# One graph-network layer on one core: the two half-block transfers of x and of the result become one, and ScalarE asks for x

## The chip, the cores and the metric

The kernel runs on one core of one Trainium2 chip. The metric is the device time of a launch in microseconds, and where several runs were made, their median. A core has five engines with instruction streams of their own: TensorE (PE; its weight loads are listed apart as PEld), VectorE (DVE), ScalarE (ACT), GpSimd (POOL) and SyncE (SP). SP, ACT and POOL can ask for transfers; the transfers themselves run on 16 DMA engines that all three share.

## The reference: what is computed

There are 12,500 nodes with 128 numbers each (`x`), and 412,500 edges with 48 numbers each (`edge_attr_48`), sorted by the node that receives them (`dst`). Cut to what matters, the reference is:

```python
h = jnp.maximum(_layernorm(x, axis=-1), 0.0)
agg = jax.ops.segment_sum(edges, dst, num_segments=12500)   # 12500 x 48
u = graph_globals[0]                                        # the same 64 numbers for all nodes
z = jnp.concatenate([h, agg, u], axis=1)
return x + (jax.nn.relu(z @ W1 + b1) @ W2 + b2)             # W1: 240 x 256, W2: 256 x 128
```

So every node is normalized, gets the sum of its edges' numbers beside it, and goes through a two-layer network; the result is added to `x`. All numbers are float32. The edges are 79.2 MB, `x` and the result 6.4 MB each.

## The kernel before, in words

**Two streams.** The edges are cut into 403 chunks of 1,024 edges (128 partitions x 8), and the chunks into two halves, the streams. A step takes one chunk of each stream; 6 steps make a group (`CG`), and there are 34 groups and 207 steps. In a step `contract` (L370) multiplies, for each of 8 edges per partition and for both streams, 48 edge columns with a one-hot matrix, which adds them up by receiver in PSUM (L377; a float32 product leaves two records in the trace, so a step shows 32). VectorE builds the one-hot matrices a group ahead (`onehot`, L365), and `add` (L393) adds a finished group into the big sums `aggT` in SBUF. Stream 0 lies on partitions 0 to 47 and stream 1 on 64 to 111.

**Node blocks.** The first 6,144 nodes belong to stream 0, and as many from node 6,356 (`END`) on to stream 1. Both are cut into 25 blocks. A block has 64 partitions (`PH`) of each stream, and each partition holds r nodes that follow one another in memory: r is 2 in the first and the last block and 4 in the other 23. So one partition's part of `x` is one run of 2 KB (1 KB where r is 2). The 212 nodes between the streams are a 26th block of 53 partitions. A block goes through these parts, which `pieces` and `parts` put between the steps: `normalization` (L483: `bn_stats` on DVE at L517, some small DVE and ACT operations, `xn` on ACT at L513), `transpose` (L524, copied to `hT` by ACT at L533), `hidden_x` and `hidden_sums` (L537 and L556, with the result taken by ACT as `hid` at L573), `output` (L577, products at L585), and `store` (L590: DVE adds `x` and the bias into `ot`, L593, and SP stores it, L598).

**Transfers.** SP asks for all edges (`load_edges`, L151): a transfer brings two chunks, and 15 buffers are filled ahead (`PF`); after that, a new load follows each pair of chunks that has been used up. SP also asks for most of `dst` (L180) and stores the results, all in one order. POOL asks for the weights, the biases and `x`. Two of the small ones tell something of how a transfer is spread: SP's very first one, `first0` (L250), fetches four numbers as a 1 x 2 x 2 pattern, and ACT's first two, `di` (L180), fetch 12 rows of 4 KB each.

**How x is asked for.** `load_x(k)` (L207) takes a buffer for a pair of blocks and puts one `load` per block on a list with the step from which it is due; there are four such buffers (`XBUFS`). `next_x` (L231) takes the next due one off the list and emits it; it is called every third step. For a block, `load` emits two transfers, one for the 64 partitions of each stream (L218). `store` does the same with the result:

```python
for s in range(2):
    nc.sync.dma_start(rows_of(out, s * END + a0, PH, nr), od[s * PH:(s + 1) * PH])
```

Before the first step, POOL asks for the first three blocks of `x` (L304, L308 and L316), between clearing `aggT` and loading the weights.

**Spare products.** `stir(n)` (L333) multiplies the identity with itself n times into a PSUM tile that nobody reads (L336). It is called with 4, 5 and 3 ahead of the first step, and in the steps before the 14th wherever no piece was taken (L741).

Of the kernel before, what the change touches and what calls it, by code (L numbers as in the profile page):

```python
# [21 lines left out]
def kernel(  # L22
# [31 lines left out]
    nc = tc.nc  # L54
    N, D = x.shape
# [32 lines left out]
    XBUFS = 4  # L88
    PH = P // 2
# [11 lines left out]
    END = MID + NM  # L101
# [67 lines left out]
    def next_edges():  # L169
        if e_loads:  # L170
            _, s, c, n = e_loads.pop(0)
            e = ep.tile([P, CL, T * DE], F32, name="e")
            load_edges(e, c, n)
            for k in range(n):
                edges[c + k] = (e[:, k], k == n - 1)

    def load_chunks(di, at, c, n, queue):

        full = max(0, min(n, NFULL - c))
        queue.dma_start(di[at:at + full], dst[c * CE:(c + full) * CE].rearrange("(c e) -> c e", e=CE))  # L180
        if full < n:
            for q in range(0, CE, TAIL):
                m = min(TAIL, CE - q)
                queue.dma_start(di[at + full:at + n, q:q + m], dst[None, E - m:E])

    def rows_of_block(b):

        return [sum(chunks[s * NI + begins[b]:s * NI + begins[b + 1]]) for s in range(2)]
# [3 lines left out]
    def load_dst(b, queue):  # L192
        di = dp.tile([P, CE], I32, name="di", bufs=2)
        at = 0
        for s, n in enumerate(rows_of_block(b)):
            load_chunks(di, at, C0[s] + begins[b] * CG, n, queue)
            at += n
        return di

    def rows_of(ap, a, m, r):  # L200

        return ap[a:a + m * r].rearrange("(p r) d -> p (r d)", p=m)

    xs, xts, xns, xbs, hTs, hids, pos = {}, {}, {}, {}, {}, {}, {}
    x_loads = []

    def load_x(k):  # L207

        if k >= len(pairs):
            return  # L210
        xt = xp.tile([P, 2, R * D], F32, name="xt")
        xts[k] = xt

        def load(i, j):
            a, m, r = blocks[j]
            if j < NB2:
                for s in range(2):
                    nc.gpsimd.dma_start(xt[s * PH:(s + 1) * PH, i, :r * D], rows_of(x, s * END + a, PH, r))  # L218
                return
            f = m - m % 16  # L220
            nc.gpsimd.dma_start(xt[:f, i, :r * D], rows_of(x, a, f, r))
            if f < m:
                nc.gpsimd.dma_start(xt[f:m, i, :r * D], rows_of(x, a + f * r, m - f, r))

        for i, j in enumerate(pairs[k]):
            xs[j] = xt[:, i].rearrange("p (r d) -> p r d", d=D)
            x_loads.append((k, lambda i=i, j=j: load(i, j), max(step, min(16 * k - 32, 114 + 4 * k))))
# [3 lines left out]
    def next_x(late=0):  # L231

        if x_loads and x_loads[0][2] <= step - late:
            k, load, _ = x_loads.pop(0)
            load()
            came[k] = step
# [11 lines left out]
    with nc.allow_non_contiguous_dma(reason="a few hundred numbers, once"):  # L248
        begin = begins[1]
        nc.sync.dma_start(  # L250
            first0, dst[:2 * C0[1] * CE].rearrange("(a s e) -> a s e", a=1, s=2)[:, :, GE // 2:begin * GE:GE])
    dis = {0: load_dst(0, nc.scalar)}
    for i in range(PF):
        next_edges()
        if i == 1:
            dis[1] = load_dst(1, nc.sync)
# [19 lines left out]
    with nc.allow_non_contiguous_dma(reason="a few hundred numbers, once"):  # L276
        for s in range(2):
            mid0 = C0[s] * CE
            n = min(NI, (E - mid0) // GE)
# [3 lines left out]
            for i in range(n, NI):  # L283
                m = mid0 + i * GE + GE // 2
# [13 lines left out]
        at += n  # L298
    for c in range(0, 2048, 1024):
        nc.gpsimd.memset(aggT[:, c:c + 1024], 0.0)  # L300
    step = -4
    for k in range(XBUFS):
        load_x(k)
    next_x()  # L304
    nc.gpsimd.memset(w1a, 0.0)
    with nc.allow_non_contiguous_dma(reason="a few hundred numbers, once"):
        nc.gpsimd.dma_start(w1h, W1[0:D])
        next_x()  # L308
        nc.gpsimd.dma_start(w1u, W1[D + DE:D + DE + G])
        nc.gpsimd.dma_start(u, graph_globals[0:1].rearrange("a g -> g a"))  # L310
        nc.gpsimd.dma_start(b1_sb, b1.rearrange("(a p) -> p a", p=P))
        nc.gpsimd.dma_start(w1a[0:DE], W1[D:D + DE])
        nc.gpsimd.dma_start(w1a[HI:K2], W1[D:D + DE])
        nc.gpsimd.dma_start(w2, W2.rearrange("(a p) d -> p a d", p=P))
        nc.gpsimd.dma_start(b2_sb, b2[None, :].to_broadcast([P, D]))
    next_x()  # L316
    for c in range(2048, NC, 1024):
        nc.gpsimd.memset(aggT[:, c:min(c + 1024, NC)], 0.0)
    least = const.tile([1, NG], F32)
# [13 lines left out]
    def stir(n):  # L333

        for _ in range(n):
            nc.tensor.matmul(spare[:, 0], ident, ident, start=True, stop=True)  # L336
# [58 lines left out]
    def first_nodes(b):  # L395

        at = 0
        for s, n in enumerate(rows_of_block(b)):
            g = s * NI + begins[b]
            m = -(-n // CG)  # L400
            nc.vector.tensor_tensor(
                brow[:, b, at:at + m * CG].rearrange("a (i k) -> a i k", k=CG),
                offs[:, None, :].to_broadcast([1, m, CG]),
                (first[:, g:g + m] if b else first0[:, s])[:, :, None].to_broadcast([1, m, CG]), OP.subtract)
            at += n
# [8 lines left out]
    def shift_dst(b, di):  # L414

        rows = rows_in[b]
        ra, rb = rows_of_block(b)
        pb = pst.tile([P, 2], F32, name="pt")
        nc.tensor.matmul(pb[:rows, 0:1], brow[:, b, :rows], one, start=True, stop=True)  # L419
        nc.tensor.matmul(pb[:rows, 1:2], (cols if b < NB - 1 else last_cols)[:, :rows], one, start=True, stop=True)  # L420
        nc.scalar.copy(base[:rows, b], pb[:rows])  # L421
        df = dp.tile([P, CE], F32, name="df", bufs=2)
        nc.scalar.activation(df[:rows], di[:rows], AF.Identity, bias=base[:rows, b, 0:1])
        return df

    def spread(b, df, parts=(0, 1), start=False):

        ra, rb = rows_of_block(b)
        if 0 in parts:
            rels[b] = dp.tile([P, IB, CG // 2, 4 * T], F32, name="rel", bufs=2)  # L430
            if b == NB - 1:
                nc.gpsimd.memset(rels[b][:, NI - 1 - begins[b]], 0.0)
        rv = rels[b].rearrange("p i h (k s t) -> p s t (i h k)", s=2, t=T)
        q = T // 2
        for t0 in [a * q for a in parts]:
            own = start and t0
            pt = turn_dst(df, ra + rb, t0, *((psh, "ph") if own else (pst, "pt")))
            nc.scalar.copy(rv[:, 0, t0:t0 + q, :ra], pt[:, :, :ra])
            (nc.vector.tensor_copy if start else nc.scalar.copy)(rv[:, 1, t0:t0 + q, :rb], pt[:, :, ra:ra + rb])  # L439
# [150 lines left out]
    def store(j):  # L590
        a0, m, nr = blocks[j]
        ot = mp.tile([P, R, D], F32, name="ot")
        nc.vector.tensor_tensor(ot[:m, :nr], pos.pop(j)[:m, :nr], xbs.pop(j)[:m, :nr], OP.add)  # L593
        k = m - m % 16
        od = ot[:, :nr].rearrange("p r d -> p (r d)")
        if j < NB2:
            for s in range(2):
                nc.sync.dma_start(rows_of(out, s * END + a0, PH, nr), od[s * PH:(s + 1) * PH])  # L598
            return
        nc.sync.dma_start(rows_of(out, a0, k, nr), od[:k])  # L600
        if k < m:
            nc.scalar.dma_start(rows_of(out, a0 + k * nr, m - k, nr), od[k:m])
# [17 lines left out]
    pieces = [(8, 0.4, lambda: turn(0)), (12, 0.8, lambda: turn(1))]  # L620
# [37 lines left out]
    def turn(j):  # L658
        nonlocal turned
        while not normalized(j):  # L660
            next_part(True)
        transpose(j)
        turned = j
# [12 lines left out]
    stir(4)  # L676
    first_nodes(0)
    dfs = {0: shift_dst(0, dis[0])}
    stir(5)
    spread(0, dfs[0], start=True)  # L680
    stir(3)
# [17 lines left out]
    for b in range(1, NB):  # L699
        i = begins[b]  # L700
# [15 lines left out]
    for step in range(CG * NI + 3):  # L716
        i, k = divmod(step, CG)
        if i < NI:
            contract(i, k)
        for f in plan.get(step, []):  # L720
            f()
        if step % 3 == 2:
            next_x(1)
        if k == 0:
            if i > 0:
                add(0, i - 1)
                add(1, i - 1)
        if k == 0:
            hots.pop(i - 1, None)
            onehot(i + 1, (0, 2))  # L730
        if k == 2:
            onehot(i + 1, (1,))
        store_late()
        for _ in range(2 if step % 2 or step < 20 else 1):
            next_part()
        credit = min(credit + 0.75, 1.2)
        n = len(pieces)
        while pieces and pieces[0][0] <= step and pieces[0][1] <= credit:
            credit -= pieces[0][1]
            pop_piece()  # L740
        if n == len(pieces) and step < 14:  # L741
            stir(1)
    while pieces:
        pop_piece()
        store_late()
# [114 lines left out]
```

## Time and profile before

| | us |
|---|---|
| median of 3 runs | 372.35 (370.56 to 373.52) |
| the profiled execution, its own time | 373.86 |
| its span, first to last instruction | 372.1 |
| PE busy | 325.3 (87%) |
| DVE busy | 242.0 (65%) |
| ACT busy | 123.8 (33%) |
| POOL busy | 42.2 (11%) |

The mean granted TensorE clock was 0.969 of full speed. The profile is of one execution; its own time stands 1.5 us above the median of the runs, and its span 1.8 us below its own time. The rows of the page say how long an engine was busy in the whole span; a row of "busy tenths" divides the span into 40 slices of 9.3 us. A group row names the line, the engine, the operation, what it writes and reads, and how often; then its busy time, the mean of one, and the idle time ahead of it with what ended most of it. Transfers are listed by queue: q1 is SP's, q10 is ACT's, q0 is POOL's, and q8 and q14 bring instructions; a packet is one run of bytes or one 4-byte receipt that a DMA engine writes when its share of a transfer is done.

### The profile page before, as it was taken

What the parts mean: (1) busy time and instruction counts of PE and PEld (TensorE: products, weight loads), DVE (VectorE), ACT (ScalarE), POOL (GpSimd) and SP (SyncE); (2) the same over time, 40 slices, a digit from 0 to 9 for tenths busy, and PEclk for the clock granted to TensorE, in tenths of its full rate; (3) what the DMA queues carried; (4) which work ended last, traced back from release to release, by engine and by line L of the source; (5) the groups of instructions that cost most, each with busy time, mean ns of one, the idle gap of its engine ahead of it and who ended that gap; (6) DMA issues with size and microseconds to landing.
All of it is one profiled execution on the core that took longest, in us unless ns stands there. A gap on an engine that the chain in (4) does not pass through costs nothing.

```text
span 372.1 us, 17860 instructions
## 1 busy us (share of the span) xinstructions
PE 325.3 (87%) x8059; PEld 261.5 (70%) x8060; DVE 242.0 (65%) x415; ACT 123.8 (33%) x296; POOL 42.2 (11%) x106
## 2 busy tenths in 40 slices
PE   7878968799986986999996986999999999999981
PEld 7766757787875765886874865777787778687661
DVE  2987555495992766776497582866868877785310
ACT  3224323085041072072242051543062335412330
POOL 9670400020020020020020020010000010000000
PEclk9997989899998999999999999999999999999996
DMA  7999999999898799899779899898889798941021
GB/s 214 307 315 307 326 304 309 307 320 315 272 306 246 233 291 285 271 296 317 227 239 313 267 282 264 267 300 261 286 256 307 238 343 269 307 150 36 21 53 29
DMA packets 62285, 95.41 MB, mean 256 GB/s; under 512 B 5277, under 2 KB 57097, under 8 KB 62198
## 3 DMA queue, kind: packets, MB, share of 16 engines
q1 hardware_dynamic: 59340, 87.16, 76.0%
q0 software_dynamic: 2800, 6.90, 7.3%
q8 instruction: 65, 1.06, 1.2%
q14 instruction: 22, 0.18, 0.2%
q10 hardware_dynamic: 58, 0.11, 0.1%
HBM read 87.74 MB, written 6.40 MB: 253 GB/s over the span
## 4 chain that ended last, share of the span: by engine, by line
PE 80%; issue 10%; DVE 5%; ACT 2%; POOL 0%; DVEq 0%; ACTq 0%; POOLq 0%
PE ps L377 40%; PE po L585 12%; PE ph L553 11%; PE ph L566 7%; PE pt L529 4%; PE po L336 3%; DVE oh L365 3%; PE pt L445 1%; ACT hid L573 1%; DVE ot L593 1%; DVE aggT L393 1%; DVE st L517 0%; ACT xn L513 0%; PE pt L419 0%; PE pt L420 0%
## 5 line engine op out<-in xcount | busy, mean ns | idle before, releaser
L377 PEld LDWEIGHTS ps<-oh,e 128*48 128x48 f32 x6448 | 180.9, 128 | 76.6 <-issue 69.7
L377 PE MATMUL ps<-oh,e 128*48 128x44 f32 (+1 forms) x6448 | 193.5, 219 | 25.4 <-issue 25.1
L365 DVE TENSOR_TENSOR oh<-iota,rel 128x2816 f32<-128x2816 f32 (+3 forms) x72 | 149.8, 2099 | 6.7 <-ACT rel L439 5.7
L573 ACT ACTIVATE hid<-ph,bias 128x256 f32<-128x256 f32 (+2 forms) x102 | 41.6, 460 | 87.7 <-PE ph L566 85.8
L393 DVE TENSOR_TENSOR aggT<-aggT,ps 48x201 f32 (+1 forms) x68 | 24.4, 359 | 65.3 <-PE ps L377 51.8
L585 PE MATMUL po<-w,hid 128*64 128x128 f32 (+1 forms) x784 | 60.9, 280 | 6.7 <-issue 6.0
L553 PE MATMUL ph<-hT,w1h 128*64 128x512 f32 (+2 forms) x208 | 55.4, 586 | 1.1 <-issue 1.1
L218 POOL DMA_DIRECT2D xt<-in_x_dram x50 | 26.0, 528 | 236.2 <-ACT xn L513 76.0
L585 PEld LDWEIGHTS po<-w,hid 128*64 128x64 f32 (+1 forms) x784 | 44.9, 138 | 9.7 <-issue 7.4
L513 ACT ACTIVATE xn<-xt,sh,sc 128x128 f32<-128x128 f32 (+1 forms) x100 | 42.7, 488 | 2.8 <-DVE sh L507 2.8
L593 DVE TENSOR_TENSOR ot<-po,xb 128x512 f32<-128x512 f32 (+2 forms) x26 | 17.4, 670 | 33.1 <-PE po L585 32.8
L566 PE MATMUL ph<-aggT,w1a 48*64 48x256 f32 (+1 forms) x400 | 32.5, 393 | 3.6 <-ACT hid L573 3.5
L503 ACT ACTIVATE sc<-va,eps 128x8 f32<-128x8 f32 (+3 forms) x15 | 4.5, 299 | 84.2 <-DVE va L502 84.2
L517 DVE BATCH_NORM_STATS2 st<-xt 128x6 f32<-128x128 f32 (+1 forms) x100 | 23.2, 279 | 0.0
L533 ACT COPY hT<-pt 128x512 f32<-128x512 f32 (+2 forms) x26 | 14.4, 554 | 16.6 <-PE pt L529 16.5
L529 PE MATMUL pt<-ident,xn 128*128 128x128 f32 (+1 forms) x100 | 17.3, 297 | 0.0
L566 PEld LDWEIGHTS ph<-aggT,w1a 48*64 48x64 f32 x400 | 10.6, 131 | 8.3 <-ACT hid L573 4.7
L547 DVE TENSOR_TENSOR xb<-xt,b_sb 128x1024 f32<-128x1024 f32 (+3 forms) x15 | 15.6, 1037 | 0.1
L553 PEld LDWEIGHTS ph<-hT,w1h 128*64 128x64 f32 x208 | 12.4, 141 | 2.5 <-issue 2.4
L336 PE MATMUL po<-ident 128*128 128x128 f32 x46 | 12.2, 402 | 2.0 <-POOL ident masks.py:199 2.0
L529 PEld LDWEIGHTS pt<-ident,xn 128*128 128x128 f32 (+1 forms) x100 | 10.9, 147 | 1.7 <-issue 0.4
L421 ACT COPY base<-pt 108x2 f32<-108x2 f32 (+3 forms) x5 | 0.8, 156 | 30.6 <-PE pt L420 30.6
(92 smaller groups left out, 101.0 us busy)
## 6 DMA issues: line engine op xcount, KB each, us to landing
e<-in_edge_attr_dram SPq DMA_DIRECT2D x200, 384.0 KB, 5.3
xt<-in_x_dram POOLq DMA_DIRECT2D x46, 128.0 KB, 7.2
out_dram<-ot SPq DMA_DIRECT2D x46, 128.0 KB, 3.2
di<-in_dst_dram SPq DMA_DIRECT2D x4, 216.0 KB
e<-in_edge_attr_dram SPq DMA_DIRECT2D x2, 192.0 KB, 4.0
di<-in_dst_dram SPq DMA_DIRECT2D x2, 180.0 KB
di<-in_dst_dram SPq DMA_DIRECT2D x2, 144.0 KB
xt<-in_x_dram POOLq DMA_DIRECT2D x4, 64.0 KB, 5.3
```

The lines of the kernel that those rows point to most:

```text
L218: nc.gpsimd.dma_start(xt[s * PH:(s + 1) * PH, i, :r * D], rows_of(x, s * END + a, PH, r))
L336: nc.tensor.matmul(spare[:, 0], ident, ident, start=True, stop=True)
L365: nc.vector.tensor_tensor(hots[i][:, at:at + n * Q * w].rearrange("p (h q w) -> p h q w", h=n, w=w)[:, :, q], iota[:, None, None, :w].to_b ...
L377: nc.tensor.matmul(ps[s * HI:s * HI + DE, o:o + WID[k]], edges[c][0][:, t * DE:(t + 1) * DE], hot(i, s, k, t), start=(k == 0 and t == 0), ...
L393: nc.vector.tensor_tensor(to, to, acc[i % len(acc)][h, :wg], OP.add)
L513: nc.scalar.activation(xns[j][:m, r], xs[j][:m, r], AF.Relu, bias=sh[:m, c:c + 1], scale=sc[:m, c:c + 1])
L517: parts.append((k, None, lambda i=i, j=j, r=r: nc.vector.bn_stats(st[:m, i * nr + r, :], xs[j][:m, r, :])))
L529: nc.tensor.transpose(pt[:, r, :m], xn[:m, r], ident[:m, :m])
L553: nc.tensor.matmul(phs[j, a][c:c + HI, :nr * m], w1h[:, a * P + c:a * P + c + HI], hTs[j], start=True, stop=False, skip_group_check=True)
L566: nc.tensor.matmul(phs[j, a][c:c + HI, s * n:(s + 1) * n], w1a[h, a * P + c:a * P + c + HI], aggT[h, f:f + n], start=False, stop=True, ski ...
L573: nc.scalar.activation(hids[j][:, a, :nr, h:f], phs[j, a][:, h * nr:f * nr].rearrange("h (p r) -> h r p", r=nr), AF.Relu, bias=bias[:, a:a ...
L585: nc.tensor.matmul(pos[j][c:k, r], hids[j][:, a, r, c:k], w2[:, a], start=(a == 0), stop=(a == NH - 1), skip_group_check=True)
```

## The change

A helper `both` describes the rows of both streams of one block as one pattern in device memory: 2 streams, `END * 128` numbers apart, by 64 partitions by one run of r x 128 numbers. With it, a block of `x` is one transfer into 128 partitions and no longer two into 64, and a block of the result one transfer out of 128 partitions. `x` is asked for by ScalarE and no longer by GpSimd. The first three blocks of `x` are no longer asked for between POOL's start-up work: their calls come after `shift_dst` of the first part of `dst`, so in ACT's order behind the first two of its operations there (L421, L423). The spare products inside the steps are dropped; the 12 ahead of the first step stay. SP still stores the results, and the 53-partition block keeps its two transfers of 48 and 5 partitions.

```diff
+    def both(ap, a, r):
+
+        return bass.AP(tensor=ap.tensor, offset=ap.offset + a * D, ap=[[END * D, 2], [r * D, PH], [1, r * D]])
+
...
             a, m, r = blocks[j]
             if j < NB2:
-                for s in range(2):
-                    nc.gpsimd.dma_start(xt[s * PH:(s + 1) * PH, i, :r * D], rows_of(x, s * END + a, PH, r))
+                nc.scalar.dma_start(xt[:, i, :r * D], both(x, a, r))
                 return
             f = m - m % 16
-            nc.gpsimd.dma_start(xt[:f, i, :r * D], rows_of(x, a, f, r))
+            nc.scalar.dma_start(xt[:f, i, :r * D], rows_of(x, a, f, r))
             if f < m:
-                nc.gpsimd.dma_start(xt[f:m, i, :r * D], rows_of(x, a + f * r, m - f, r))
+                nc.scalar.dma_start(xt[f:m, i, :r * D], rows_of(x, a + f * r, m - f, r))
...
     dis = {0: load_dst(0, nc.scalar)}
+    step = -4
+    for k in range(XBUFS):
+        load_x(k)
...
-    step = -4
-    for k in range(XBUFS):
-        load_x(k)
-    next_x()
     nc.gpsimd.memset(w1a, 0.0)
...
         nc.gpsimd.dma_start(w1h, W1[0:D])
-        next_x()
         nc.gpsimd.dma_start(w1u, W1[D + DE:D + DE + G])
...
-    next_x()
     for c in range(2048, NC, 1024):
...
         if j < NB2:
-            for s in range(2):
-                nc.sync.dma_start(rows_of(out, s * END + a0, PH, nr), od[s * PH:(s + 1) * PH])
+            nc.sync.dma_start(both(out, a0, nr), od)
             return
...
     dfs = {0: shift_dst(0, dis[0])}
+    for _ in range(3):
+        next_x()
     stir(5)
...
-        n = len(pieces)
         while pieces and pieces[0][0] <= step and pieces[0][1] <= credit:
             credit -= pieces[0][1]
             pop_piece()
-        if n == len(pieces) and step < 14:
-            stir(1)
```

## The prediction

> **What bounds the kernel now.** I read the engines and the 40 slices of the page first, then the queues, then the chain that ended last, and then what SP waits for.
>
> ```profile
> span 372.1 us, 17860 instructions
> PE 325.3 (87%) x8059; PEld 261.5 (70%) x8060; DVE 242.0 (65%) x415; ACT 123.8 (33%) x296; POOL 42.2 (11%) x106
> DMA  7999999999898799899779899898889798941021
> GB/s 214 307 315 307 326 304 309 307 320 315 272 306 246 233 291 285 271 296 317 227 239 313 267 282 264 267 300 261 286 256 307 238 343 269 307 150 36 21 53 29
> ...
> q1 hardware_dynamic: 59340, 87.16, 76.0%
> q0 software_dynamic: 2800, 6.90, 7.3%
> q8 instruction: 65, 1.06, 1.2%
> ...
> PE 80%; issue 10%; DVE 5%; ACT 2%; POOL 0%; DVEq 0%; ACTq 0%; POOLq 0%
> ```
>
> The chain is TensorE's: 80% of the span is products, and 10% "issue", pauses in which PE waits for nothing the profile shows. But the row DMA stands at 8 or 9 tenths until slice 35 (some 330 us): the 16 DMA engines are nearly as full as PE, and they are this full only because the load is spread evenly. The shares of the queues add up to 85% of 16 engines' span, so each is busy for some 316 us. POOL, which asks for x now, is idle for nearly nine tenths.
>
> ```profile
> SPq L151 <- PE ps L377: 138.2, 131, 3.4
> SPq L151 <- DMA e<-in_edge_attr_dram: 26.6, 30, 2.2
> ```
>
> SP waits mostly for PE to free an edge buffer (in total, times, longest): PE sets the pace, by a small margin.
>
> **The change, part by part.**
>
> *How many DMA engines a transfer uses.* This decides the case, and the trace counts it: each participating engine writes a 4-byte receipt. The first 2.45 us (queue: packets, MB, share):
>
> ```profile
> q10 hardware_dynamic: 24, 0.05, 7.8%
> q1 hardware_dynamic: 6, 0.00, 0.1%
> ```
>
> ACT's first `di` transfer has 12 rows of 4 KB (0.05 MB); 24 packets are 12 rows and 12 receipts, so 12 engines. SP's `first0` fetches four numbers as 1 x 2 x 2; 6 packets are 4 numbers and 2 receipts: two engines. Two stores of 64 partitions, 361 to 364.9 us:
>
> ```profile
> q1 hardware_dynamic: 160, 0.13, 14.0%
> ```
>
> These are 128 rows and 32 receipts, 16 engines each. So the first dimension longer than 1 sets the number: 12, 2 and 64 gave 12, 2 and 16. But in all of these both sides begin with the same count. The new pattern doesn't: SBUF begins with 128 partitions, device memory with 2 streams. The Trainium skill (DMA: Bandwidth & Descriptors, "Why a DMA increments its semaphore by 16 and not by 1") says that the largest number up to 16 is taken that divides the slowest dimension of both sides; for 128 and 2 that is **two engines**, the lowest-numbered, always the same pair. The same page ("Rules for kernel authors") advises one 128-partition transfer in place of two halves, and no row here tells which of the two holds for this pattern. By the advice the sum is about 370 us, by the first rule about 565. I take the first rule, since it speaks of both patterns and the trace agrees with it wherever it can be counted.
>
> *Sum on the two engines.* The 25 blocks hold 6.29 MB of x (6.40 without the 212 middle nodes' 0.11), and the results as much: 12.58 MB over two engines, **6.29 MB each**. The rest stays spread: q1 without those results 80.87 MB, q0 without x 0.61, instructions and small ones 1.35; 82.8 / 16 = **5.18 MB each**. Together 11.47 MB. Rate of a busy engine: q1's 87.16 MB in 0.760 x 16 x 372.1 = 4,525 us is 19.3 GB/s, with all 16 crowding the memory. The fastest slice, 343 GB/s over 16, gives 21.4, and slices in a finer cut (100 to 320 us in 5.5 us each) reach 373:
>
> ```profile
> GB/s 347 283 292 181 232 239 335 241 316 285 273 299 258 373 232 162 262 283 353 243 279 341 216 274 288 257 309 270 244 328 268 250 246 333 287 195 350 294 315 258
> ```
>
> or 23.3. So 11.47 MB take 594 us at 19.3 and 492 at 23.3. With 14 engines half idle the crowd is thinner (95 MB in 560 us are 170 GB/s in place of 256), so I take 22: **521 us**. The other engines need 5.18 MB, some 240 us. To this come: 2.7 us before the first edges move; some 8 us for the last block after the last load (332 to 372 us is 40 us now, but mostly products that overlap the queue's rest); and times in which the two engines have nothing queued, since SP waits for a buffer or for `ot`, or ACT is late with x. 15 edge buffers are 15 steps, 1.8 blocks, so I put the last at 6%, 31 us: an estimate. 521 + 3 + 8 + 31 = 563 us of span, and with the 1.8 us between span (372.1) and own time (373.86) **565 us**. The profiled execution lies 1.5 us over the median of the runs, which is nothing at this size.
>
> *What becomes late.* Every edge transfer has a share on the two slow engines and is complete only with it, so all edges arrive at their pace: a step (384 KB, 24 KB per engine, 1.1 us at 22 GB/s) plus a block's 512 KB over 8.2 steps, 11.6 us per block: 20.8 us a block, where the span now gives 372 / 25.9 = 14.4. PE then waits for edges, which it hardly does now.
>
> *The issues.* SP's stores:
>
> ```profile
> L598 SPq DMA_DIRECT2D out_dram<-ot x50: 466/574/1577, 54.0 to 361.9; - x50
> ```
>
> 25 fewer by 0.574 us are 14.4 us of SP, and lie under its 138 us of waiting: nothing. POOL loses 52 issues, 52 x 0.528 = 27 us, under its idleness: nothing; what stands behind them there (weights, the clearing of `aggT`) comes some 3 us earlier, and nobody waits for it but one `add` for 0.7. ACT gains 27 issues (25 blocks, two for the middle). ACT's own two cost 0.304 and 0.609, so 8 to 16 us on an engine that is busy for a third, if the queue takes them at once. It need not:
>
> ```profile
> 3.51 15.45 SPq L151 DMA_DIRECT2D e<-in_edge_attr_dram  x15
> ```
>
> ```profile
> L151 SPq DMA_DIRECT2D e<-in_edge_attr_dram x202: 346/368/3407, 1.7 to 326.6; - x101
> ```
>
> The first row is the timeline (start, us), the second the durations in ns (min, median, max): fifteen issues, of 0.368 us in the median, took 1.03 each at the start and up to 3.4 later: a full queue holds the engine that issues. On ACT, `hid`, `hT`, `xn` and the one-hot inputs `rel` stand behind a held issue, and PE behind these. With 16 engines I'd take 0.5 us; with two, a block's 64 rows per engine take 6 us alone and 12 beside edges. This is in the 6%, and worse is a rival. At the start the three first issues stand behind `df` (ends 5.66 us) and before `rel` (7.33): 3 x 0.456 = 1.4 us fit; at SP's 1.03 each they'd be 1.4 us late. A later x load also waits until DVE's `xb` (L547) has read its buffer, a wait that moves from POOL to ACT, with the same operations behind it; it is emitted only after that `xb`, so the wait is at most about one `xb` (1.04 us) for each of 11 pairs, and less where DVE is ahead. I take 0 for it and keep the 11 us as an end.
>
> *The spare products.*
>
> ```profile
> L336 PE MATMUL po<-ident x46: 275/421/583, 2.0 to 32.3; 128*128 128x128 f32 x46
> ```
>
> 46 records are 23 products; 12 stay. Eleven pairs of some 0.49 us (timeline) are 5.4 us of PE between 10 and 33 us. Best case 5 us gained; none if DVE's one-hot work is the limit (busy 9.79 of the 10 us from 10 to 20); and a loss of some 2 us if the clock, which is granted at 0.83 from 20 to 40 us, falls further. I take 2 gained, and in the forecast 0: there the edges set the pace.
>
> **The rivals.**
>
> *A: ScalarE is held, and its hold adds to PE's time.* If both x transfers of a pair hold ACT until the two engines have drained them, that is 2 x 12 us per pair; PE needs 2 x 14.4 and can go on without ACT for only part of it. In turn: 53 us a pair, 12.5 pairs, 660 us, and with start and end 670 to 700. For it speaks the 3.4 us hold of SP; against it that the edges run into free buffers meanwhile, so the two engines lose little.
>
> *B, the other side: the transfers use 16 engines.* Then the bytes and their spread are as now, all issues are hidden, and what remains is 2 us of spare products gained and up to 1.5 us of late ACT at either end: 368 to 370, between 363 (all spare products, x earlier) and 382 (clock, held issues, waits for `xb`). It decides as soon as the pattern is split along its 64 or 128 rows in place of the 2 streams. For it speaks the advice above; against it `first0`'s two receipts. It is also the case in which the change does what it says, and shows how little: POOL and SP were not what the end waited for.
>
> *C: two engines, but the rate is higher or lower*: the ends 492 and 594 with 2% and 8% idle give 515 to 655; this is the likeliest case's own range.
>
> **How the numbers follow.** Two engines with the two as the bound (C included): 0.70. A: 0.12. B: 0.15. Something slower still, over 710: 0.03. The predicted time is the first case's, 565. From 500 to 700 lies nearly all of the first and most of A: 0.69 + 0.11 = 0.80. About 1% is what a measurement of this kernel can tell from no change (its three runs lie 0.8% apart). Only B can end near or under it: 0.06 faster, 0.06 same, 0.03 slower; so slower is 0.88.
>
> **What would show it.** Right: the share of the DMA engines falls to about 0.5 to 0.6 with some 170 GB/s through the whole span, q10 carries 6.4 MB, x comes as 3,200 rows with 50 receipts, in place of 400 for 25 transfers on 16 engines; PE waits for edges (L377 for the DMA) for over 100 us; landing of edges, 5.3 us now, and of results, 3.2 us, grows several times. Wrong: 16 receipts per x transfer, a DMA row of 8 and 9 tenths, and a span within 2% of 372. For A: ACT's issues of 5 us and more each, and PE's waits on `hid` instead of edges.

## The result

The changed kernel takes **485.98 us** (median; 484.25 to 487.17), the kernel before 372.44 beside it: a ratio of 1.305, 95% interval 1.299 to 1.312. (Some executions of a kernel are a little slower than the rest; the medians are over all of them, the ratios here and below over the faster ones alone.) The direction and the cause were as forecast, two DMA engines; the size was not: 565 us was predicted, and the range began at 500.

The page of the changed kernel, for the lines shown of before (busy times, DMA share in 40 slices of 12.1 us, queues, the chain that ended last):

```profile
span 484.1 us, 17713 instructions
PE 341.8 (71%) x8037; PEld 272.4 (56%) x8038; DVE 242.6 (50%) x415; ACT 123.6 (26%) x296; POOL 15.5 (3%) x54
DMA  8729594993566565765655765594665767786111
GB/s 240 252 80 268 175 290 123 318 301 122 184 207 199 198 183 190 244 229 172 210 177 175 234 201 196 179 313 140 197 206 171 237 204 221 218 253 237 56 40 43
...
q1 hardware_dynamic: 58590, 87.16, 57.4%
q10 hardware_dynamic: 3382, 6.51, 3.6%
...
DMA 56%; PE 32%; ACT 4%; DVE 3%; issue 1%; ACTq 1%; SPq 1%; POOL 0%; DVEq 0%; POOLq 0%
```

As many bytes move, but the mean share of the DMA engines is down to 5 to 7 tenths over most of the span, and the chain is no longer TensorE's: 56% of it is transfers. The packets of q10 count out: 24 rows of `di` with 24 receipts, 3,200 + 53 rows of x, 5 rows of the result with 5 receipts and 16 + 5 receipts for the middle block make 3,332; the 50 left are **two receipts for each of 25 transfers**. How that looks in time, from 183 to 195 us in 40 slices of 0.3 us:

```profile
DMA  5799999921111111111118769964172689869479
GB/s 135 220 352 372 377 394 398 329 91 67 55 55 55 41 55 55 55 41 55 55 55 123 131 224 362 358 224 135 55 101 77 169 323 387 318 162 229 106 287 384
```

For nearly 4 us the share stands at 1 tenth, which is 2 of 16 (0.125), and mostly 41 to 55 GB/s move: two engines finish what was asked of them while the other 14 have nothing. Over the eleven slices of 55 and 41 in a row the mean is 52 GB/s, so each of the two does about 26 alone.

### The profile page after: what moved, and what is told of

It is laid out like the page before. It is cut to its first block, busy times and chain, and to the rows that moved or that the text cites. A ratio compares the mean times of both kernels' runs of the same rounds, so it can differ in the third digit from the quotient of the medians.

```text
span 484.1 us, 17713 instructions
## 1 busy us (share of the span) xinstructions
PE 341.8 (71%) x8037; PEld 272.4 (56%) x8038; DVE 242.6 (50%) x415; ACT 123.6 (26%) x296; POOL 15.5 (3%) x54
## 3 DMA queue, kind: packets, MB, share of 16 engines
q8 instruction: 65, 1.06, 0.9%
## 4 chain that ended last, share of the span: by engine, by line
DMA 56%; PE 32%; ACT 4%; DVE 3%; issue 1%; ACTq 1%; SPq 1%; POOL 0%; DVEq 0%; POOLq 0%
DMA e<-in_edge_attr_dram 45%; PE ps L377 17%; DMA xt<-in_x_dram 6%; PE po L585 6%; PE ph L553 5%; DMA out_dram<-ot 4%; PE ph L566 3%; DVE oh L365 2%; ACT xn L513 2%; ACT hid L573 1%; PE pt L529 1%; ACTq L221 1%; SPq L151 1%; DVE ot L593 0%; PE po L336 0%
## 5 line engine op out<-in xcount | busy, mean ns | idle before, releaser
L377 PEld LDWEIGHTS ps<-oh,e 128*48 128x48 f32 x6448 | 189.1, 133 | 85.7 <-issue 49.7
L377 PE MATMUL ps<-oh,e 128*48 128x44 f32 (+1 forms) x6448 | 198.8, 224 | 31.6 <-DMA e<-in_edge_attr_dram 20.0
L585 PE MATMUL po<-w,hid 128*64 128x128 f32 (+1 forms) x784 | 66.6, 295 | 26.2 <-ACT hid L573 26.0
L513 ACT ACTIVATE xn<-xt,sh,sc 128x128 f32<-128x128 f32 (+1 forms) x100 | 42.9, 485 | 112.9 <-DMA e<-in_edge_attr_dram 96.1
L585 PEld LDWEIGHTS po<-w,hid 128*64 128x64 f32 (+1 forms) x784 | 49.9, 148 | 29.0 <-ACT hid L573 27.9
L566 PE MATMUL ph<-aggT,w1a 48*64 48x256 f32 (+1 forms) x400 | 36.0, 421 | 34.3 <-ACT hid L573 28.4
L553 PE MATMUL ph<-hT,w1h 128*64 128x512 f32 (+2 forms) x208 | 58.5, 633 | 0.0
L529 PE MATMUL pt<-ident,xn 128*128 128x128 f32 (+1 forms) x100 | 19.6, 303 | 22.9 <-ACT xn L513 13.7
L517 DVE BATCH_NORM_STATS2 st<-xt 128x6 f32<-128x128 f32 (+1 forms) x100 | 23.6, 281 | 22.5 <-DMA xt<-in_x_dram 22.5
L445 PE MATMUL pt<-ident,df 108*128 108x108 f32 (+3 forms) x36 | 6.6, 312 | 9.8 <-ACT hT L533 9.7
L445 PEld LDWEIGHTS pt<-ident,df 108*128 108x128 f32 (+3 forms) x36 | 4.9, 203 | 10.6 <-ACT hT L533 9.8
L438 ACT COPY rel<-pt 128x216 f32<-128x216 f32 (+3 forms) x9 | 4.0, 444 | 20.2 <-issue 10.9
```

Of the source, the lines that this page charges most:

```text
L377: nc.tensor.matmul(ps[s * HI:s * HI + DE, o:o + WID[k]], edges[c][0][:, t * DE:(t + 1) * DE], hot(i, s, k, t), start=(k == 0 and t == 0), ...
L513: nc.scalar.activation(xns[j][:m, r], xs[j][:m, r], AF.Relu, bias=sh[:m, c:c + 1], scale=sc[:m, c:c + 1])
L517: parts.append((k, None, lambda i=i, j=j, r=r: nc.vector.bn_stats(st[:m, i * nr + r, :], xs[j][:m, r, :])))
L529: nc.tensor.transpose(pt[:, r, :m], xn[:m, r], ident[:m, :m])
L553: nc.tensor.matmul(phs[j, a][c:c + HI, :nr * m], w1h[:, a * P + c:a * P + c + HI], hTs[j], start=True, stop=False, skip_group_check=True)
L566: nc.tensor.matmul(phs[j, a][c:c + HI, s * n:(s + 1) * n], w1a[h, a * P + c:a * P + c + HI], aggT[h, f:f + n], start=False, stop=True, ski ...
```

## The experiments

Each kernel is told by its difference from the changed kernel (E4 and E5: from the one before). "Halves" are two transfers of 64 partitions per block. The ratio is to runs of the kernel before on the same chip (medians 369.0 to 373.0 us).

| run | what it is | us | ratio to before, 95% |
|---|---|---|---|
| E1 | x and results in halves | 370.7 | 0.994 (0.990 to 0.997) |
| E2 | only x in one transfer | 428.7 | 1.148 (1.137 to 1.158) |
| E3 | only the results in one | 387.8 | 1.040 (1.031 to 1.049) |
| E4 | before, both in one, x by GpSimd | 398.2 | 1.067 (1.057 to 1.077) |
| E5 | before, fewer spare products | 371.0 | 1.001 (0.996 to 1.005) |
| E6 | E2, x by SyncE | 425.2 | 1.140 (1.129 to 1.151) |
| E7 | x by SyncE, both in one | 499.2 | 1.339 (1.326 to 1.352) |
| E8 | 2 of 8 products | 482.4 | 1.293 (1.280 to 1.305) |
| E9 | E2 with 2 of 8 | 413.9 | 1.125 (1.120 to 1.130) |
| E10 | E3 with 2 of 8 | 386.2 | 1.048 (1.042 to 1.054) |
| E11 | E1 with 2 of 8 | 323.4 | 0.878 (0.869 to 0.887) |
| E12, E13, E15 | E1, 4, 8, 2 groups that touch | 369.9, 371.2, 373.8 | 1.004 (1.001 to 1.007), 1.002 (0.998 to 1.005), 1.011 (1.000 to 1.022) |
| E14 | E1 and an unread copy of x | 478.6 | 1.298 (1.289 to 1.307) |
| E16 | E1, x in 2 groups apart | 432.8 | 1.168 (1.155 to 1.181) |
| E17 | E1, x in 4 groups apart | 388.2 | 1.043 (1.035 to 1.052) |
| E18 | E1, x in 8 groups apart | 373.0 | 373.0 us before beside it |

My theory was that the bytes on the two engines set the time; the main rival, that ScalarE is held while its queue takes an x transfer, and TensorE with it.

**E1, the pattern undone.**

```diff
-                nc.scalar.dma_start(xt[:, i, :r * D], both(x, a, r))
+                for s in range(2):
+                    nc.scalar.dma_start(xt[s * PH:(s + 1) * PH, i, :r * D], rows_of(x, s * END + a, PH, r))
...
-            nc.sync.dma_start(both(out, a0, nr), od)
+            for s in range(2):
+                nc.sync.dma_start(rows_of(out, s * END + a0, PH, nr), od[s * PH:(s + 1) * PH])
```

> The changed kernel with only the pattern undone: x and the results go again as two transfers of 64 partitions each, x still asked for by ScalarE, spare products still dropped. Two-engine theory (the time comes from the bytes that fall on the same two DMA engines): all load is spread again, so 366 to 376 us, the share of the DMA engines back at 8 and 9 tenths, and 16 receipts per transfer. Rival, ScalarE is held by asking for x, or the late x at the start costs: most of the 113 us stay, over 420 us.

370.7 us, and q10 has 16 receipts for each half (E1, queues):

```profile
q10 hardware_dynamic: 4132, 6.51, 6.7%
```

So all 113 us come from the pattern. ScalarE asking for x, the later first requests and the dropped spare products together cost and bring nothing to speak of. That holds for the late start too: here six requests of half a block took 9.05 us, and ScalarE's first `rel` came at 15.33 us, about as late as in the changed kernel (waits of ACT, E1):

```profile
ACT rel L439 <- DMA xt<-in_x_dram: 9.7, 1, 9.7
```

**E2 and E3, one direction each** (one of E1's two edits each).

> The changed kernel with the results stored in halves again; only x comes as one transfer. Two-engine theory: x's 3.15 MB and 5.57 MB of the spread rest are 8.7 MB on each of the two engines; at the 24.2 GB/s that the changed kernel reached (11.47 MB in some 474 us) that is 360 us, as much as TensorE needs, so 372 to 395 us. Rival, ScalarE held by x transfers that drain slowly: the hold is as in the changed kernel, so over 430 us, and far above the kernel in which only the results are one transfer.

> The changed kernel with x in halves again (asked for by ScalarE); only the results are one transfer. Two-engine theory: the same bytes on the two engines as in the kernel with only x in one transfer, so about the same time, 372 to 395 us, the two within 10 us of each other. Rival, ScalarE held: no hold is left, so within 1% of the kernel with all in halves.

428.7 and 387.8 us. E3 is where the byte sum put it. E2 is not: 57 us over the 372 that began its range, although the same 8.7 MB fall on the two engines. The sum of bytes alone failed here, and the rival was not out.

**E4, x by GpSimd** (before with both patterns).

```diff
-                for s in range(2):
-                    nc.gpsimd.dma_start(xt[s * PH:(s + 1) * PH, i, :r * D], rows_of(x, s * END + a, PH, r))
+                nc.gpsimd.dma_start(xt[:, i, :r * D], both(x, a, r))
...
-            for s in range(2):
-                nc.sync.dma_start(rows_of(out, s * END + a0, PH, nr), od[s * PH:(s + 1) * PH])
+            nc.sync.dma_start(both(out, a0, nr), od)
```

> The kernel before with only the pattern changed: x and the results as one transfer of 128 partitions each, but x still asked for by GpSimd where it was, and the spare products kept. Two-engine theory: the same bytes on two engines if GpSimd's transfers follow the same rule, 475 to 495 us. Rival, ScalarE held: GpSimd can be held without harm, so the x part of the loss goes away and it ends below 430 us.

398.2 us, 10 over E3. It looked like the rival's, but it tells less than I had meant. In its packet records x's packets run mostly two to four at a time, with up to two transfers under way; ScalarE's in the changed kernel hardly ever more than two. So GpSimd's transfers are narrow too, but probably not always on the same pair, as the Trainium skill has it for this path (DMA: Bandwidth & Descriptors, "Why a DMA increments its semaphore by 16 and not by 1": consecutive engines from a cursor that moves on). The trace doesn't name the engines. GpSimd's transfers also report to semaphores of their own, which matters below (E9 to E11), and that difference was not taken apart from the first. So E4 doesn't decide.

**E5, the spare products alone** (from the kernel before).

```diff
-        if n == len(pieces) and step < 14:
-            stir(1)
```

> The kernel before with only the spare products in the steps dropped. If TensorE's chain is what they lengthen: up to 5 us faster, 367 to 370 us. If VectorE's one-hot work sets the pace there, or the clock falls: 371 to 374 us.

371.0 us, 1.001 of before: no difference.

**E6 and E7, x by SyncE** (from E2 and from the changed kernel).

```diff
-                nc.scalar.dma_start(xt[:, i, :r * D], both(x, a, r))
+                nc.sync.dma_start(xt[:, i, :r * D], both(x, a, r))
```

> As the kernel with only x in one transfer (428.7 us), but asked for by SyncE in place of ScalarE; the results in halves. The 58 us over the kernel with all in halves (370.7 us) are more than the bytes on two engines explain (8.7 MB at 24 GB/s are 360 us). Theory of the hold (ScalarE stands still while its queue takes the 64 rows per engine, and TensorE waits for it): SyncE can be held without TensorE waiting for ScalarE, so 372 to 400 us. Rival, x itself comes too late or the edges beside it do, whoever asks: 415 to 440 us.

> The changed kernel (486.0 us) with x asked for by SyncE; both patterns as in the change. Theory of the bytes: 11.47 MB on each of two engines at the best packet rate, 24 GB/s, are 475 us and nothing can hide them: 475 to 495 us. Theory of the hold: what ScalarE's standing still added is gone, 455 us or less.

425.2 and 499.2 us; E7 ends 4 us above the range that the bytes gave it. With no x request on ScalarE, E6 is 3.5 us faster than E2 and E7 13 us slower than the changed kernel, so ScalarE need not be held for the time to be lost. That alone doesn't clear the rival, for now x itself comes late: VectorE's first operation on it (`st`) waits 156.8 us for x in E7 and 22.5 in the changed kernel. E8 decides.

**E8, three quarters of the edge products left out.**

```diff
-        for t in range(T):
+        for t in (0, T - 1):
             for s, g, c in groups:
                 nc.tensor.matmul(
```

> The changed kernel, but of the 8 products per chunk and stream only the first and the last are made: the sums by receiver leave out three quarters of the edges. All transfers stay, and TensorE loses some 145 us of its 342. Theory of the bytes: the two engines set the time whatever TensorE does, 465 to 486 us. Theory of the hold (TensorE's work and ScalarE's standing still in turn): 430 us or less.

482.4 us, 3.6 less than the changed kernel, though PE's busy time went from 341.8 to 270.8 us at a lower granted clock (0.719 against 0.868):

```profile
PE 270.8 (56%) x3201; PEld 181.3 (38%) x3202; DVE 241.9 (50%) x415; ACT 123.3 (26%) x296; POOL 15.4 (3%) x54
```

If TensorE's work, or ScalarE's hold added to it, had set the time, much of these 71 us would have gone. So TensorE and its clock don't set the time of the changed kernel; the transfers do, and the rival falls. The packet records agree: from 10 to 470 us of the changed kernel, fewer than two packets are under way for only 1.7 us.

**E9, E10, E11, the same quarter of the products on E2, E3 and E1.**

> Only x in one transfer (asked for by ScalarE), and of the 8 products per chunk and stream only the first and the last: three quarters of the edges are left out of the sums, all transfers stay. If the 428.7 us of that kernel are the two engines' time too (they then move 8.7 MB at about 20 GB/s, slower than the 24 in the changed kernel), it stays at 415 to 430 us. If the excess over 360 us comes from x or ScalarE being late for TensorE's work, it falls to 360 to 400 us.

> Only the results in one transfer, x in halves, the same quarter of the products. The same 8.7 MB on the two engines: at 24 GB/s 360 to 375 us. If a result's bytes cost the two engines less than x's (their reads are from SBUF and not from device memory), clearly under the kernel with only x in one transfer: 340 us or less. If TensorE set the 387.8 us, it falls too.

> All in halves on 16 engines with the same quarter of the products: the floor of the spread transfers. 95.4 MB at the 343 GB/s of the fastest slice are 278 us, at the mean of the busy stretch (277 GB/s) 344 us; with some 10 us at the ends and the last block's products 295 to 360 us. If it stays at 370, the DMA engines bound the kernel before as well.

413.9, 386.2 and 323.4 us; E9 ends 1 us under its range for the two engines, E10 11 us over. With all in halves the transfers can be done in 323 us, so before the change they had at least some 47 us to spare under TensorE's time (370.7 - 323.4). With less work for TensorE, 386 of 388 us stay with the results on two engines, 414 of 429 with x on two engines, and 482 of 486 with both. So E2's excess is not TensorE's work either: all but 15 us of it stay. The same bytes cost 28 us more as x than as results. In the packet records the stretches with just two packets under way differ by about as much: 62.6 us in E9, 38.1 in E10. Results are hardly faster in themselves: two engines alone move 48 GB/s of x in E9 (281 to 287 us) and 51 of results in E10 (355.5 to 361.5 us).

Where they go can be read at SP, which asks for the edges (waits of SP: total, times, longest; E2, then E3, then E1):

```profile
SPq L151 <- DMA xt<-in_x_dram: 101.1, 18, 8.8
...
SPq L598 <- DMA xt<-in_x_dram: 23.3, 6, 5.9
```

```profile
SPq L151 <- DMA out_dram<-ot: 36.7, 15, 3.4
```

```profile
SPq L151 <- DMA xt<-in_x_dram: 2.2, 3, 1.2
```

In E2 SP stands for 124 us until an x transfer is through, in E3 for 37 us until a result is, and in E1, with x in halves, for 3 us. ScalarE stands too. In the changed kernel (timeline; the bracket is idle time):

```profile
5.42 11.10 ACTq L221 DMA_DIRECT2D xt<-in_x_dram  x3
16.56 0.24 ACT L438 COPY rel<-pt 128x48 f32<-128x48 f32 x1 [10.90 <-issue]
...
210.58 0.51 ACTq L221 DMA_DIRECT2D xt<-in_x_dram  x1
211.20 0.88 ACT L513 ACTIVATE xn<-xt,sh,sc 128x128 f32<-128x128 f32 x2 [8.90 <-DMA e<-in_edge_attr_dram]
```

The first three x requests take 11.1 us; the third of them stands for 7.6 us. Later ones wait for something else. A transfer reports its end to a semaphore, a counter that engines can wait on. In the instruction records the transfers of SP and of ScalarE take eight semaphores in turn, all from one set, and a request waits until the transfer that had its semaphore before is complete, whoever asked for it. The x request at 210.58 us has that of an edge transfer issued at 199.57, whose last receipt came at 210.56; those at 142.10, 159.58, 179.94 and 216.12 us followed the end of an earlier transfer as closely, within 0.03 us. In E2, SP's edge load at 213.04 us waits in the same way for an x transfer of ScalarE that was issued at 194.01 and complete at 212.98. So a slow transfer holds later requests of both engines, and ScalarE's `xn` stands behind them (waits of ACT, the changed kernel and then E1):

```profile
ACT xn L513 <- DMA e<-in_edge_attr_dram: 96.1, 11, 16.3
```

```profile
ACT xn L514 <- DMA e<-in_edge_attr_dram: 2.6, 2, 1.6
```

While SP stands, for such a semaphore or for a buffer that PE has not used up yet, no new edges are asked for, and the 1-tenth stretches follow. That SP's standing makes the 28 us is read from waits and packets, not isolated by a run; one with separate semaphores for x would tell.

**E12, E13, E15: 4, 8 and 2 groups in each half, for x and results.**

```diff
+    def split(ap, a, r):
+        n = PH // 4
+        return bass.AP(tensor=ap.tensor, offset=ap.offset + a * D, ap=[[n * r * D, 4], [r * D, n], [1, r * D]])
```

> All in halves, but each half's rows in device memory written as 4 groups of 16 rows, so that the pattern begins with 4. If the first counts of both sides set the engines: 4 receipts per transfer, 5.18 + 12.58/4 = 8.33 MB on the busiest engines, at 23 to 24 GB/s and 10 us for the ends 357 to 372 us, which is TensorE's time too: 372 to 392 us. If only the total of rows counts: 370 us as with all in halves.

> The same with 8 groups of 8 rows. First counts: 8 receipts, 5.18 + 12.58/8 = 6.75 MB, some 300 us on the busiest engines, hidden under TensorE: 367 to 377 us. Otherwise 370 us too, so only the receipts tell these apart here.

> The same with 2 groups of 32 rows: still two transfers of 64 partitions per block, but each on two engines, so the same 11.47 MB on each of them as in the change. If the number of engines is all that matters: 475 to 500 us. If it is the one transfer of 128 partitions, or the distance between the two streams' rows: 370 us.

369.9, 371.2 and 373.8 us, and all three have 4,132 packets on q10, as E1: groups that follow one another without a gap were joined into one run of rows, and the transfers used 16 engines. They tell nothing of 2, 4 or 8 engines. They do repeat E1, at 1.004, 1.002 and 1.011 of before: E1's 0.994 is no gain to build on.

**E14, an unread copy** (E1, and each block of x a second time over two engines into a buffer nobody reads).

```diff
+        xd = xp.tile([P, R * D], F32, name="xd")
...
+                nc.scalar.dma_start(xd[:, :r * D], both(x, a, r))
```

> All in halves on 16 engines, and beside it a second copy of each block of x, as one transfer over two engines, asked for by ScalarE into a buffer that nothing reads. 9.1 MB on the two engines. If the 28 us between only x (413.9 us) and only the results (386.2 us) are the slower rate at which the two engines take x, it is as slow here: 420 us or more. If they come from x being late for those who read it, it is gone: 380 to 408 us.

478.6 us: 108 over E1, more than the 58 of E2. VectorE never waits for x here, so x needn't be late for the pattern to cost time. But the bytes alone don't make all of it: 9.1 MB on each of the two engines at 24.2 GB/s are 376 us. SP stands for the copy as it stood for x in E2, 93.6 us in all, and ScalarE's first `rel` waits 27.4 us behind three more requests (waits of SP and of ACT):

```profile
SPq L151 <- DMA xd<-in_x_dram: 84.6, 16, 9.2
...
SPq L601 <- DMA xd<-in_x_dram: 9.0, 1, 9.0
```

```profile
ACT rel L441 <- DMA xt<-in_x_dram: 27.4, 1, 27.4
```

So its size isn't to be compared with E2's; how much each of these costs was not taken apart.

**E16, E17, E18: groups that cannot be joined, x only.** The groups lie one node closer than they should, so later groups hold their neighbours' nodes and the kernel no longer computes the layer; the amounts of bytes stay. With 2, 4 and 8 for k:

```diff
+    def split(ap, a, r):
+        n = PH // k
+        return bass.AP(tensor=ap.tensor, offset=ap.offset + a * D, ap=[[(n * r - 1) * D, k], [r * D, n], [1, r * D]])
...
-                    nc.scalar.dma_start(xt[s * PH:(s + 1) * PH, i, :r * D], rows_of(x, s * END + a, PH, r))
+                    nc.scalar.dma_start(xt[s * PH:(s + 1) * PH, i, :r * D], split(x, s * END + a, r))
```

> All in two halves of 64 partitions, results on 16 engines; only the pattern of x in device memory begins with 2: two groups of 32 rows, one node less apart than they should be, so that they cannot be joined into one run of 64 rows (the second group of each half then holds its neighbours' nodes; the amount is the same). Number of engines: 2 receipts per transfer and the same bytes on the two engines as with only x in one 128-partition transfer (428.7 us): 415 to 440 us. Form (one transfer of 128 partitions over two distant streams): 370 us.

> The same with four groups of 16 rows, each one node less apart. Number of engines: 4 receipts, 5.57 + 6.29/4 = 7.14 MB on the busiest engines, some 300 to 330 us at 22 to 24 GB/s and so mostly hidden: 370 to 385 us.

> The same with eight groups of 8 rows. Number of engines: 8 receipts, 6.36 MB on the busiest engines, hidden: within 1% of all in halves (370.7 us).

432.8, 388.2 (3 us over its range) and 373.0 us. The queue q10 of the three:

```profile
q10 hardware_dynamic: 3432, 6.51, 4.4%
```

```profile
q10 hardware_dynamic: 3532, 6.51, 5.7%
```

```profile
q10 hardware_dynamic: 3732, 6.51, 6.3%
```

Without the other 3,332 packets that are 100, 200 and 400 receipts for 50 transfers: 2, 4 and 8 engines. E16 with its halves of 64 partitions lies within 1% of E2 with one transfer of 128. So neither the single transfer nor the distance of the streams matters, only the number of engines, and for x it goes 432.8, 388.2, 373.0, 370.7 us with 2, 4, 8 and 16.

## Why the prediction was right in its cause and wrong in its size

*Two engines*: right, and settled by the receipts, E1 and E16 to E18. For sides that begin with 128 and 2 the rule of both sides' first counts held, and the advice to make one transfer of 128 partitions did not (both from the page of the Trainium skill cited in the prediction).

*The bytes*, 11.47 MB on each of the two: the trace doesn't name the engines, but the stretch shown above has both kinds on one pair. From 186 to 189 us a block of x (packets from 183.9 to 194.4 us) and a result (complete at 194.25) are both moving, at some 26 GB/s each, and the share is that of 2 engines, not of 4. The costs add accordingly: over E11's 323 us, x costs 91 (E9) and the results 63 us (E10), and both together 159 (E8); on two pairs the larger would cover the smaller.

*The rate* is **the step that failed**, with the idle share that was added to it. I put a busy engine between 19.3 and 23.3 GB/s and took 22. With some 10 us of the 484 left for the two ends, 11.47 MB in 474 us are 24.2 GB/s, above my upper end, and 47 us less than the 521. Two engines alone do 24 to 26 each: 52 GB/s for two in the stretch above, 48 in E9. The rate could have been read from the kernel before. Its row of bytes from 196 to 205 us in slices of 0.225 us:

```profile
GB/s 278 255 182 221 264 298 237 298 209 234 223 246 193 203 212 255 323 319 300 273 300 396 362 396 364 387 471 344 382 389 362 371 410 373 391 421 376 410 416 376
```

The last 19 slices, 4.3 us, have a mean of 389 GB/s, or 24.3 for each of 16 engines that all work. My 23.3 came from slices of 5.5 us, which hold slower moments as well; my 19.3 divided bytes by packet times, and these overlap: from 10 to 40 us they add up to 1.06 of the 16 engines' time. So 23.3 was no bound: at its best a busy engine of the kernel before does what the two engines of the changed kernel do over the whole span. Why it does less in the first half of this row, with the share at 9 tenths all along, no run shows; that the crowd of 16 slows it, as I assumed for the 22, stays open.

*The idle share*: I added 6%, 31 us, for times in which the two have nothing queued. They hardly have such times: fewer than two packets are under way for 1.7 of the 460 us between 10 and 470 us. The two terms, 47 us from the rate and 31 from the idle share, are 78 of the 79 us between 565 and 486.

*What becomes late*: I had expected PE to wait for edges for over 100 us. Edges themselves account for 20.0 of PE's waits; most of them came through ScalarE (waits of PE):

```profile
PE ph L566 <- ACT hid L573: 28.4, 8, 14.7
PE po L585 <- ACT hid L573: 26.0, 4, 15.0
PE ps L377 <- DMA e<-in_edge_attr_dram: 20.0, 12, 5.0
```

The hold of rival A is real, 8.7 us at a time ahead of `xn` (96.1 / 11), but except at the start it comes from the shared semaphores. It doesn't add to the time, because the two engines work meanwhile (E8). The two signs that I gave for a queue that holds its engine don't show one: the fifteen issues of 15.45 us contain waits for these semaphores, and SP's 3.4 us is its longest wait for PE to free an edge buffer. The start was mis-sized as well: three requests took 11.1 us, not 1.4 to 3.1, and `rel` came at 16.56 us in place of 7.33; by E1 that costs nothing.

*The issues, the wait for `xb` and the spare products*: nothing, as taken for the forecast (E1, E5); the 2 us that rival B counted as a gain did not show.

## What to carry to other kernels

Before two transfers are merged into one, look at the first count of both sides' patterns: a leading 2 in device memory put each block's 256 KB on two engines, and the whole kernel ran at their pace. Count receipts in the packets of a queue; it takes one line of the profile. And take the rate that a busy engine can reach from the shortest slices of the profile, since means over several microseconds hide it.

## What had not been expected

A slow transfer can hold an engine that never asked for it: with x on two engines SP, which asked only for edges and results, stood 124 us behind ScalarE's x transfers (E2), because both engines' transfers take their semaphores from one set. Groups of rows that touch are joined before the transfer is laid out, so a leading 2, 4 or 8 written by hand had no effect (E12, E13, E15) until the groups no longer touched (E16 to E18).
